# Counting a graph's edges: windows of 64 targets replaced by a stretch of 58 keys that moves with the chunks

## The chip, the cores and the metric

The kernel runs on one core of one Trainium2 chip. TensorE multiplies matrices into PSUM, VectorE and ScalarE work on tiles in SBUF and PSUM, GpSimd fills constants and issues some of the transfers, SyncE issues most of them. The metric is the device time of one execution in microseconds.

## The reference

There are 625 nodes with 1024 features and 20,000 edges, sorted by their target `dst`; each edge has a source `src` and one of two types. A relational graph layer is followed by a layer of routed experts:

```python
n   = t5_norm(layernorm(x)) * ln_weight
out = n @ W_root + bias
for r in range(2):
    sums = segment_sum((n[src] @ W_rel[r]) * (type == r), dst)
    cnt  = segment_sum(type == r, dst)
    out  = out + sums / max(cnt, 1)
x = x + layernorm(x) + elu(out) @ wo
x = x + experts(layernorm(x))    # 2 shared, top 2 of 8 routed, hidden 256
```

## The kernel before

The kernel gathers no edge. It builds the matrix of counts, how many edges of type r run from node s to node d, and multiplies it with the projected nodes. So the graph layer has three parts on TensorE, interleaved in one instruction stream.

**Counting.** The edges go in 160 chunks of 125 (`EC`, `EP`). `edge_columns` (L660 to L688) turns the loaded rows `ety_i`, `dst_i` and `src_i` into columns: it forms the key 640 * type + dst (L663), casts src (L662), transposes both on TensorE (`p_edge`, L669) and lets ScalarE and VectorE write three values of each edge, doubled into pairs, into `cols`: the source within its tile of 125 nodes, the key, and 16 to the power of minus the source's tile. `count_windows` (L823) takes groups of up to four chunks. VectorE makes `ohs` for a group, a one-hot row of 128 columns for each edge's source (L846), times that power (L847), and `ohk`, a one-hot row of keys (L850), by comparison with `iotk`, an iota of 1280 keys. The keys are cut into ten windows of 64 targets, 128 keys with both types (`WD`, `NW`). As edges are sorted by target, `BAND` names for each chunk the one or two windows that its targets can be in, with a slack of 384 edges. For each chunk and window TensorE loads the chunk's `ohs` as weights and adds `ohk` into the window's PSUM bank `cnt` (L859). When a window is complete, `count_out` (L803) scales it to integers on ScalarE (`xi`), splits the five source tiles packed in each number by a mask on VectorE (`ct`, L808), and casts them to bf16 on ScalarE into `CT` (L812, one copy for each type).

**Projecting.** `to_columns` transposes the normalised rows of a tile (`p_t`, L787) into `nT`. `project` (L875) multiplies a tile by one of three weights: 8 k-steps, which the profile records as 16 matmuls (`p_pr`, L880). The first five calls make the root part; the other ten are split into three bf16 parts each in `P` (ScalarE L884 and L887, VectorE L888). These need `stats` (L745) and `scales` (L763), the layernorm of a tile.

**Aggregating.** `aggregate(d, r)` (L893) multiplies `CT` and `P` for target tile d and type r, 15 matmuls (`p_agg`, L898), followed by a short chain on ScalarE and VectorE (L900 to L904); `elu(d)` and `elu_columns(d)` (`p_elT`, L929) prepare it for `output_proj` (`p_y`, L941 and L945).

**The order of the work.** After each chunk, `between(c)` emits what the table `after` (L971 to L1002) lists: projections, aggregations and the rest have chunk numbers written out by hand. A scheduler then orders each engine's instructions by its own estimate of when they become ready, and `tc.issue_after` holds an instruction behind another one of its engine. Each engine works through its own list in order. Ahead of the counting stand 24 and 40 warm-up matmuls (`warm`, L959) and, on GpSimd, in the order of the source: `ident`, the iotas `iota` (L558) and `iotk` (L562), more constants, the small loads `cb`, `vec`, `rb_t`, `bd` and `rw_t` (L609 to L645), and the memsets of `P` and `zero`. Eight buffers of `ohs` and `ohk` let VectorE run ahead of TensorE.

PSUM has eight banks: five for `acc` (windows and projections) and three for `mm`.

Behind the graph layer come `gate`, `route`, the experts and the output; they read only the node rows.

Of the kernel before, what the change touches and what calls it, by code (L numbers as in the profile page):

```python
# [11 lines left out]
I32 = mybir.dt.int32  # L12
# [18 lines left out]
WD = 64  # L31
NW = 10
ND = NW * WD
SH = 313
PACK = 4096
ROUND = 1.5 * 2.0**23
SLACK = 384
BAND = [
    (max(0, (EP * c - SLACK) >> 11), min(NW - 1, (EP * c + EP - 1 + SLACK) >> 11))
    for c in range(EC)  # L40
]
# [411 lines left out]
def sparse_kernel(  # L453
# [32 lines left out]
    psum = ctx.enter_context(tc.tile_pool(name="psum", bufs=1, space=bass.MemoryType.PSUM))  # L486
# [6 lines left out]
    def ps_acc(name):  # L493
        return psum.tile([128, 512], F32, tag="acc", name=name, bufs=5)

    def ps_mm(name):
        return psum.tile([128, 512], F32, tag="mm", name=name, bufs=3)
# [52 lines left out]
    for r in range(R):  # L550
# [5 lines left out]
    KEYS = R * ND  # L556
# [3 lines left out]

    iotk = fbig.tile([128, KEYS], F16, name="iotk")
    nc.gpsimd.iota(iotk, pattern=[[WD, NW], [ND, R], [1, WD]], base=0, channel_multiplier=0,  # L562
                   allow_small_or_imprecise_dtypes=True)
# [92 lines left out]

    SP_, KW_, VV_ = range(3)
    cols = fbig.tile([EP, 3, EC, 2], F16, name="cols")

    def edge_columns():  # L660
        rowf = fbig.tile([EH, 2, 2 * EP], F32, name="rowf")
        nc.vector.tensor_copy(rowf[:, 0], rows_i["src"])  # L662
        nc.vector.scalar_tensor_tensor(rowf[:, 1], rows_i["ety"], float(ND), rows_i["dst"],  # L663
                                       op0=ALU.mult, op1=ALU.add)
# [137 lines left out]
    CT = cbig.tile([TP, NT, KEYS], BF16, name="CT")  # L802
    def count_out(w, acc):  # L803
        xi = crow.tile([TP, R * WD], I32, tag="xi", name=f"xi_{w}")
        nc.scalar.activation(xi, acc[:TP, : R * WD], AF.Copy, scale=256.0)
        five = [TP, NT, R * WD]
        ct = crow.tile(five, I32, tag="ct", name=f"ct_{w}")
        nc.vector.tensor_tensor(ct, xi[:, None, :].to_broadcast(five),  # L808
                                mask[:, :, None].to_broadcast(five), op=ALU.bitwise_and)
        for r in range(R):  # L810
            o = CT[:, :, r * ND + w * WD : r * ND + (w + 1) * WD]
            nc.scalar.copy(o, ct[:, :, r * WD : (r + 1) * WD])  # L812


    GROUP = 4
    groups = []
    for c in range(EC):
        if groups and len(groups[-1]) < GROUP and BAND[groups[-1][0]] == BAND[c]:
            groups[-1].append(c)
        else:  # L820
            groups.append([c])

    def count_windows(between):  # L823
        accs = {}
        for cs in groups:
            c0, g = cs[0], len(cs)
            lo, hi = BAND[c0]
            kn = (hi - lo + 1) * 128
            oh_s = oneh.tile([EP, GROUP, 128], F16, tag="oh_s", name=f"ohs_{c0}")
            oh_k = oneh.tile([EP, GROUP, 256], F16, tag="oh_k", name=f"ohk_{c0}")  # L830

            def both(what, n):
                return [EP, g, n // 2, 2], cols[:, what, c0 : c0 + g][:, :, None, :].to_broadcast([EP, g, n // 2, 2])

            def halves(v):
                return v.rearrange("p g (a b) -> p g a b", b=2)

            order = ExitStack()
            if c0 == 0:
                order.enter_context(tc.issue_after(ahead.ins))  # L840
            elif c0 == 2 * GROUP:
                order.enter_context(tc.issue_after(second[0].ins))
            shape, key = both(SP_, 128)
            row = iota[:EP].rearrange("p (a b) -> p a b", b=2)
# [3 lines left out]
            shape, key = both(KW_, kn)  # L848
            row = iotk[:EP, lo * 128 : lo * 128 + kn].rearrange("p (a b) -> p a b", b=2)
            nc.vector.tensor_tensor(halves(oh_k[:, :g, :kn]), row[:, None].to_broadcast(shape), key,  # L850
                                    op=ALU.is_equal)
            order.close()
            for i, c in enumerate(cs):
                for w in range(lo, hi + 1):
                    first = c == 0 or BAND[c - 1][1] < w
                    last = c == EC - 1 or BAND[c + 1][0] > w
                    if first:
                        accs[w] = ps_acc(f"cnt_{w}")
                    nc.tensor.matmul(accs[w][:, : R * WD], oh_s[:, i, :],  # L859
                                     oh_k[:, i, (w - lo) * 128 : (w - lo + 1) * 128],  # L860
                                     start=first, stop=last)
                    if last:
                        count_out(w, accs.pop(w))
                between(c)

# [27 lines left out]
    def aggregate(d, r):  # L893
        p = ps_mm(f"p_agg_{d}_{r}")
        at = r * ND + d * TP
# [102 lines left out]
    for d, cs in enumerate(((70, 117), (78, 121), (106, 128), (138, 146))):  # L998
        for r in range(R):
            at(cs[r], aggregate, d, r)  # L1000
        at(cs[1], elu, d)
        at(cs[1] + 8, elu_columns, d)  # L1002

    def between(c):
        for f, args in after[c]:
            if f is to_columns:
                args = (args[0], hs[args[0]], *args[2:])
            f(*args)

    count_windows(between)  # L1010
    front.close()

# [10 lines left out]
    for s in range(NT + 2):  # L1023
# [15 lines left out]
        if s == 0:  # L1039
            elu_columns(NT - 1)  # L1040
# [460 lines left out]
```

## Time and profile before

| | us |
|---|---|
| three timed runs, median (lowest to highest) | 310.69 (310.52 to 311.41) |
| the profiled execution, own time | 312.2 |
| its span, first to last instruction | 310.0 |
| TensorE busy, matmuls | 297.6 (96%) |
| VectorE busy | 180.7 (58%) |
| ScalarE busy | 110.1 (36%) |
| first matmul of the counting / of the gate | 9.49 / 141.77 |

In the page's table of slices a digit is an engine's busy share in tenths of 1/40 of the span (7.75 us). In a timeline a row gives the start, the duration, the engine, the line, the operation, the tiles written and read, the number of instructions merged into it, and in brackets the idle time ahead and what ended it. Matmuls are pipelined: the time between the starts of two of them is less than the duration that is shown for one. A row of a group in the page has total busy time, then the mean duration in ns, then the idle time of the engine ahead of the group's instructions with what ended it.

### The profile page before, as it was taken

The page shows a single profiled execution, that of the slowest core. Times are in us where ns is not written, and L with a number is a line of the kernel's source. Part 1 is how long each engine was busy: PE and PEld are TensorE (multiplying, and loading weights), DVE is VectorE, ACT ScalarE, POOL GpSimd, SP SyncE. Part 2 cuts the span into 40 slices and gives each one's busy share as a digit, 9 for nine tenths or more (in the row PEclk, how much of TensorE's full clock was granted, in tenths as well). Part 3 has the DMA queues.
Part 4 walks back from the last instruction along what each step waited for, and adds up shares of the span by engine and source line. Part 5 has one row for each costly group of instructions (what it writes and reads, how often), then busy time and mean ns, then how long its engine had stood idle before and what let it go on. Part 6 is the DMA issues. An engine that isn't in the chain of part 4 may idle for free.

```text
span 310.0 us, 4844 instructions
## 1 busy us (share of the span) xinstructions
PE 297.6 (96%) x1693; PEld 200.9 (65%) x1693; DVE 180.7 (58%) x541; ACT 110.1 (36%) x248; POOL 46.7 (15%) x98
## 2 busy tenths in 40 slices
PE   8799999999999999999999999999999999999991
PEld 7577777887888763456777798877854334444451
DVE  4899999977879676873895032122214211256920
ACT  3456123432436245333424145456459421000000
POOL 9600000000000012431112032120002232200000
PEclk9999999999999999999999999999999999999999
DMA  7999900000000499999999843421047555579351
GB/s 235 306 317 401 406 31 0 3 0 2 0 0 2 126 345 303 388 390 388 319 342 408 349 147 127 137 76 62 0 135 305 218 209 200 201 285 374 154 161 45
DMA packets 27409, 61.18 MB, mean 197 GB/s; under 512 B 2175, under 2 KB 16006, under 8 KB 27374
## 3 DMA queue, kind: packets, MB, share of 16 engines
q1 hardware_dynamic: 21806, 43.77, 39.8%
q0 software_dynamic: 5280, 16.69, 14.9%
q10 hardware_dynamic: 294, 0.35, 0.5%
q8 instruction: 16, 0.26, 0.4%
q14 instruction: 13, 0.11, 0.1%
HBM read 42.76 MB, written 18.81 MB: 199 GB/s over the span
## 4 chain that ended last, share of the span: by engine, by line
PE 78%; DVE 14%; DMA 3%; ACT 1%; issue 1%; SPq 1%; ACTq 0%
PE p_h L1337 12%; PE p_yj L1395 12%; PE p_pr L880 11%; PE p_o L1450 11%; PE p_sh L1115 10%; PE p_y L941 5%; PE p_agg L898 4%; DMA xh<-in_x_dram 3%; PE p_x L1318 3%; DVE ohk L850 2%; PE p_t L787 2%; DVE ohs L847 2%; DVE ohs L846 2%; PE cnt L859 2%; PE p_y L945 1%; DVE ct L808 1%
## 5 line engine op out<-in xcount | busy, mean ns | idle before, releaser
L880 PE MATMUL p_pr<-wg,nT 128*125 128x286 f32 x240 | 61.9, 408 | 0.0
L880 PEld LDWEIGHTS p_pr<-wg,nT 128*125 128x125 f32 x240 | 43.4, 187 | 11.9 <-ACT nT L793 0.4
L1337 PE MATMUL p_h<-w1a,xsT 128*128 (+2 forms) x176 | 40.0, 380 | 0.0
L1395 PE MATMUL p_yj<-w2a,hjT 128*128 (+2 forms) x88 | 38.6, 594 | 0.0
L1450 PE MATMUL p_o<-sw,shT 128*125 128x512 f32 (+1 forms) x88 | 36.1, 553 | 0.0
L1115 PE MATMUL p_sh<-h2T,sw 128*128 128x313 f32 (+1 forms) x128 | 35.2, 428 | 0.0
L1337 PEld LDWEIGHTS p_h<-w1a,xsT 128*128 128x128 f32 (+2 forms) x176 | 28.7, 168 | 7.4 <-issue 0.5
L1115 PEld LDWEIGHTS p_sh<-h2T,sw 128*128 128x128 f32 x128 | 23.7, 189 | 8.6 <-issue 0.2
L1395 PEld LDWEIGHTS p_yj<-w2a,hjT 128*128 128x128 f32 (+2 forms) x88 | 14.4, 168 | 22.4 <-issue 22.1
L1450 PEld LDWEIGHTS p_o<-sw,shT 128*125 128x125 f32 x88 | 16.4, 187 | 16.9 <-issue 16.2
L1399 DVE COPY ys<-p_yj 128x512 f32<-128x512 f32 x15 | 10.4, 692 | 28.7 <-PE p_yj L1395 27.1
L1341 DVE COPY hj<-p_h 128x256 f32<-128x256 f32 x11 | 4.7, 425 | 31.1 <-PE p_h L1337 31.1
L850 DVE TENSOR_TENSOR ohk<-iotk,cols 125x512 f16<-125x512 f16 (+4 forms) x49 | 22.3, 455 | 0.0
L846 DVE TENSOR_TENSOR ohs<-iota,cols 125x512 f16<-125x512 f16 (+3 forms) x49 | 18.2, 372 | 6.5 <-PE cnt L859 6.5
L898 PE MATMUL p_agg<-P,CT 125*125 125x287 bf16 x150 | 20.4, 286 | 0.2 <-DVE P L888 0.2
L955 POOL DMA_DIRECT2D x1d<-xh x10 | 5.3, 533 | 101.6 <-DVE xh L948 101.2
L859 PE MATMUL cnt<-ohk,ohs 125*128 125x128 f16 x223 | 17.9, 219 | 2.8 <-DVE ohs L847 2.8
L859 PEld LDWEIGHTS <-ohs 125*128 125x128 f16 x223 | 14.6, 98 | 7.8 <-DVE ohs L847 4.2
L941 PE MATMUL p_y<-wo_t,eT 128*125 128x512 f32 x40 | 19.2, 603 | 0.0
L898 PEld LDWEIGHTS <-CT 125*125 125x125 bf16 x150 | 18.4, 136 | 0.1
L1403 POOL DMA_INDIRECT yt<-ys,row x11 | 10.8, 984 | 50.5 <-DVE ys L1399 50.5
L847 DVE TENSOR_TENSOR ohs<-ohs,cols 125x512 f16<-125x512 f16 (+3 forms) x49 | 18.1, 369 | 0.0
(295 smaller groups left out, 421.7 us busy)
## 6 DMA issues: line engine op xcount, KB each, us to landing
w1a<-in_L_ffn_W_dram SPq DMA_DIRECT2D x8, 1024.0 KB, 10.9
w2a<-in_L_ffn_W_dram SPq DMA_DIRECT2D x8, 1024.0 KB, 5.1
yt<-zero SPq DMA_DIRECT2D x2, 2560.0 KB
g<-yt SPq DMA_DIRECT2D x10, 512.0 KB, 7.7
sw<-in_L_ffn_sW_dram SPq DMA_DIRECT2D x4, 1024.0 KB, 5.5
x<-x1d SPq DMA_DIRECT2D x5, 500.0 KB
wg<-in_L_gnn_W_rel_dram SPq DMA_DIRECT2D x2, 1144.0 KB, 19.6
x1d<-xh POOLq DMA_DIRECT2D x5, 448.0 KB, 6.2
```

The source lines that it names most:

```text
L846: nc.vector.tensor_tensor(os, row[:, None].to_broadcast(shape), key, op=ALU.is_equal)
L847: nc.vector.tensor_tensor(os, os, both(VV_, 128)[1], op=ALU.mult)
L850: nc.vector.tensor_tensor(halves(oh_k[:, :g, :kn]), row[:, None].to_broadcast(shape), key, op=ALU.is_equal)
L859: nc.tensor.matmul(accs[w][:, : R * WD], oh_s[:, i, :], oh_k[:, i, (w - lo) * 128 : (w - lo + 1) * 128], start=first, stop=last)
L880: nc.tensor.matmul(p[:TP, :F], nT[:, k, m * TP : (m + 1) * TP], wg[:, k, r, :], start=(k == 0), stop=(k == KD - 1))
L898: nc.tensor.matmul(p[:TP, : F + 1], CT[:, m, at : at + TP], P[:, m, r, i], start=(m == 0 and i == 0), stop=(m == NT - 1 and i == 2))
L941: nc.tensor.matmul(ps[s][:TP, :], eT[:, k, :], wo_t[:, k, s * 512 : (s + 1) * 512], start=(k == 0), stop=False)
L1115: nc.tensor.matmul(p[:, : z - a], sw1[:, i, k, t * 128 : (t + 1) * 128], h2T[:, k, a:z], start=(k == 0), stop=(k == KD - 1))
L1337: nc.tensor.matmul(p[a:b, :H], xsT[j][:, k, a:b], w1m[j, a][:, 0, k, :] if a else w1a[:, bass.ds(e, 1), k, :], start=(k == 0), stop=(k == ...
L1395: made = nc.tensor.matmul(p[a:b], hjT[:, j, k, a:b], w2m[j, a, k][:, at] if a else w2a[:, bass.ds(e, 1), k, at], start=(k == 0), stop=(k = ...
L1403: sent.append(nc.gpsimd.indirect_dma_start(out=yt, out_offset=bass.IndirectOffsetOnAxis(ap=row[:, j : j + 1], axis=0), in_=y, in_offset=No ...
L1450: nc.tensor.matmul(p[:TP, :n], shT[:, i, k, own], sw2[:, i, k, at], start=(i == 0 and k == 0), stop=False)
```

## The change

- A chunk's keys become 2 * (dst - LOW[c]) + type, where `LOW[c]` is the lowest target that the slack allows in chunk c. They lie in a stretch of 58 (`KR`), so `iotk` goes and `iota` serves both comparisons. The chunk's offset `low` is made in the kernel: an iota on GpSimd and three small operations on VectorE; `edge_columns` subtracts it.
- One-hot rows are made for eight chunks in a call, except in the first four calls, which keep four.
- The counts lie in three PSUM banks, for two, two and one target tiles; a bank holds 250 keys of each tile. A bank is started by a matmul of a zeroed row (`nil`) over all 512 columns. A chunk adds its 58 columns to one bank, or to two where it crosses a border. `count_out` is called when a bank is complete, twice for each tile (63 and 62 targets).
- `CT` is laid out by 625 targets of each type; the copies into it read every second element of `ct`.
- While the counting runs, PSUM has three `acc`, three `mm` and two `cnt` banks; then the pool is closed and opened again with five and three.
- Some chunk numbers of aggregations and elu columns change; the elu columns of tile 3 move behind the counting.

```diff
+LOW = [max(0, (EP * c - SLACK) // DEG) for c in range(EC)]
+SPAN = (EP - 1 + 2 * SLACK) // DEG + 2
+GROUPS = (4,) * 4 + (8,) * 18
...
-    psum = ctx.enter_context(tc.tile_pool(name="psum", bufs=1, space=bass.MemoryType.PSUM))
+    banks_of = ExitStack()
+    psum, nacc = [banks_of.enter_context(tc.tile_pool(name="psum", bufs=1, space=bass.MemoryType.PSUM))], [3]
...
-    iotk = fbig.tile([128, KEYS], F16, name="iotk")
-    nc.gpsimd.iota(iotk, pattern=[[WD, NW], [ND, R], [1, WD]], base=0, channel_multiplier=0,
-                   allow_small_or_imprecise_dtypes=True)
+    KR = 2 * SPAN
...
+    low = fbig.tile([EH, 2, 2], F32, name="low")
+    nc.gpsimd.iota(low[:, 0], pattern=[[EP, 2]], base=-SLACK, channel_multiplier=2 * EP,
+                   allow_small_or_imprecise_dtypes=True)
+    nc.vector.tensor_scalar(low[:, 1], low[:, 0], 1.0 / DEG, 0.5 / DEG - 0.5, op0=ALU.mult, op1=ALU.add)
+    nc.vector.tensor_scalar(low[:, 1], low[:, 1], ROUND, -ROUND, op0=ALU.add, op1=ALU.add)
+    nc.vector.tensor_scalar(low[:, 1], low[:, 1], 0.0, 2.0, op0=ALU.max, op1=ALU.mult)
...
     def edge_columns():
         rowf = fbig.tile([EH, 2, 2 * EP], F32, name="rowf")
+        two = [EH, 2, EP]
+        nc.vector.tensor_tensor(rowf[:, 0].rearrange("c (j p) -> c j p", j=2),
+                                rows_i["ety"].rearrange("c (j p) -> c j p", j=2),
+                                low[:, 1][:, :, None].to_broadcast(two), op=ALU.subtract)
+        nc.vector.scalar_tensor_tensor(rowf[:, 1], rows_i["dst"], float(R), rowf[:, 0],
+                                       op0=ALU.mult, op1=ALU.add)
         nc.vector.tensor_copy(rowf[:, 0], rows_i["src"])
-        nc.vector.scalar_tensor_tensor(rowf[:, 1], rows_i["ety"], float(ND), rows_i["dst"],
-                                       op0=ALU.mult, op1=ALU.add)
...
-    CT = cbig.tile([TP, NT, KEYS], BF16, name="CT")
-    def count_out(w, acc):
...
+    CT = cbig.tile([TP, NT, R * N], BF16, name="CT")
+    def count_out(d, n, acc):
...
+            nc.scalar.copy(CT[:, :, r * N + d : r * N + d + n], ct.rearrange("p t (d r) -> p t d r", r=R)[:, :, :, r])
+
+    nil = fbig.tile([1, 512], BF16, name="nil")
+    nc.gpsimd.memset(nil, 0.0)
+    MAXG = max(GROUPS)
+    ends = [R * TP * min(DB * (b + 1), NT) for b in range((NT + DB - 1) // DB)]
...
-            shape, key = both(KW_, kn)
-            row = iotk[:EP, lo * 128 : lo * 128 + kn].rearrange("p (a b) -> p a b", b=2)
-            nc.vector.tensor_tensor(halves(oh_k[:, :g, :kn]), row[:, None].to_broadcast(shape), key,
+            shape, key = both(KW_, KR)
+            nc.vector.tensor_tensor(halves(oh_k[:, :g, :]), row[:, None, :SPAN].to_broadcast(shape), key,
                                     op=ALU.is_equal)
...
-                for w in range(lo, hi + 1):
...
-                    nc.tensor.matmul(accs[w][:, : R * WD], oh_s[:, i, :],
-                                     oh_k[:, i, (w - lo) * 128 : (w - lo + 1) * 128],
-                                     start=first, stop=last)
+                a, z = R * LOW[c], R * min(LOW[c] + SPAN, N)
+                for b, end in enumerate(ends):
...
+                    if first:
+                        accs.append(psum[0].tile([128, 512], F32, tag="cnt", name=f"cnt_{b}", bufs=2))
+                        nc.tensor.matmul(accs[b], nil[:, :128], nil, start=True, stop=False)
...
+                    nc.tensor.matmul(accs[b][:, f - base : t - base], oh_s[:, i, :], oh_k[:, i, f - a : t - a],
+                                     start=False, stop=last)
...
-    for d, cs in enumerate(((70, 117), (78, 121), (106, 128), (138, 146))):
+    for d, cs in enumerate(((70, 114), (78, 119), (133, 137), (141, 150))):
...
     count_windows(between)
     front.close()
+    banks_of.close()
+    psum[0] = ctx.enter_context(tc.tile_pool(name="psum2", bufs=1, space=bass.MemoryType.PSUM))
+    nacc[0] = 5
...
-        if s == 0:
-            elu_columns(NT - 1)
+        if s < 2:
+            elu_columns(NT - 2 + s)
```

## The prediction

> **What bounds the kernel now.** I read the page's table of slices first: TensorE is at 9 or more tenths in almost every slice, so time is lost or won in TensorE's own queue. Then the timelines of TensorE, VectorE and GpSimd over the first 145 us, the stage that the change touches; the gate (p_gate, 141.8 us) and all behind it stay as they are.
>
> ```profile
> PE   8799999999999999999999999999999999999991
> ...
> DVE  4899999977879676873895032122214211256920
> ...
> L859 PE MATMUL cnt<-ohk,ohs 125*128 125x128 f16 x223 | 17.9, 219 | 2.8 <-DVE ohs L847 2.8
> ```
>
> A matmul's "mean" is latency, so I take pitches, start to start. Groups of cnt matmuls run at 55.8 ns (37 in 2.23 us, 0.22 of it the last one's tail); a projection of 16 records takes 3.91 us; 15 p_agg take 1.87; 8 transposes p_t 0.87. Summed by stretch:
> - 9.5 to 38.8 us: 5 projections 19.55, 40 p_t 4.4, 48 cnt 2.7, p_vec 0.1: 26.7 of 29.3 us, so 2.6 of waits.
> - 38.8 to 94.65: 10 projections 39.1, 5 aggregations 9.35, 123 cnt 6.9: 55.3 of 55.85.
> - 94.65 to 141.8: 52 cnt 2.9, 5 aggregations 9.35, p_elT 1.7, p_y 22.45, p_t 2.0, the closing layernorm chain 6.2: 44.6 of 47.15, so 2.5 of waits.
>
> VectorE is full from 20 to 62 us and the chain of waits often runs through it, but TensorE's queue is full beside it. So count matmuls are worth their pitch, VectorE's work almost nothing, and a later start its whole length less what it fills of the 2.6 us.
>
> **The start.** First the GpSimd, VectorE and TensorE timelines (start us, duration, engine, line):
>
> ```profile
> 1.44 1.34 POOL L562 IOTA iotk<- 128x1280 f16 x1
> ...
> 4.90 0.75 POOL L609 DMA_DIRECT2D cb<-in_L_gnn_conv_bias_dram  x1
> ...
> 9.20 0.36 POOL L618 TENSOR_TENSOR join<-ident 128x32 f32<-128x32 f32 x1
> 12.28 0.55 POOL L624 DMA_DIRECT2D bd<-in_L_ffn_sb_dram  x1 [2.72 <-DMA cb<-in_L_gnn_conv_bias_dram]
> ...
> 13.80 0.95 POOL L645 DMA_DIRECT2D rw_t<-in_L_ffn_rW_dram  x1
> 14.74 0.25 POOL L869 MEMSET P<- 125x30 bf16 x1
> ```
> ```profile
> 3.24 0.41 DVE L663 SCALAR_TENSOR_TENSOR rowf<-ety_i,dst_i 80x250 f32<-80x250 int32 x1 [1.54 <-DMA dst_i<-in_dst_dram]
> 3.58 0.28 DVE L662 CAST rowf<-src_i 80x250 f32<-80x250 int32 x1
> ```
> ```profile
> 1.28 2.74 PE L961 MATMUL scrap<-iota 128*128 128x128 f16 x24 [1.28 <-POOL iota L558]
> 4.00 1.10 PE L669 MATMUL p_edge<-ident,rowf 80*125 80x80 f32 x4
> 5.03 0.23 PE L730 MATMUL p_lnw<-ident,lnw 8*128 8x8 f32 x1
> 5.19 2.41 PE L961 MATMUL scrap<-iota 128*128 128x128 f16 x40
> 9.49 0.40 PE L859 MATMUL cnt<-ohk,ohs 125*128 125x128 f16 x4 [1.89 <-DVE ohs L847]
> ```
>
> The edge keys now need `low`, an iota on GpSimd that the source places after all the small loads. In the instruction order of the changed kernel as built, it stands behind the rw_t load, where the memset of P stood (14.74), and the memset of `nil` behind it. GpSimd works in order, and its bd load still waits for cb's landing. With iotk gone, what precedes moves up by 1.27 us (1.44 to 2.71): cb is issued at 3.63, and, if it again takes 7.38 us until GpSimd goes on, lands at 11.0. From there to the slot are 2.46 us (12.28 to 14.74): `low` starts at 13.5 and ends at about 13.65.
>
> On VectorE the three steps on `low` stand ahead of the key row. Three dependent small operations: 0.195 us each (L709 to L713 start at 123.20, 123.40, 123.59, 123.79), 0.6. The new subtraction (nearest row L663, 0.41, plus about 0.04 for dependence) 0.45, the key again 0.45, the src cast and the handover to TensorE 0.4. So p_edge starts at about 15.55 instead of 4.00: **11.5 us later**. Behind it stand, in order, q, the first statistics, ahead of the first one-hot rows, h, p_t, every projection. All of it moves; nothing on TensorE can be taken ahead but the 64 warm-up matmuls and the two `nil` matmuls.
>
> Ends for the landing: had GpSimd not to wait at all, it would reach bd at 8.3 (9.56 less 1.27), `low` would end at 10.95, and the delay would be 8.8; if cb lands at 12.28 as before, 12.8. I keep 11.5, since the GpSimd loads from 4.9 to 8.7 us, 4 bytes to 140 KB, all took 6.4 to 7.2 us.
>
> The Trainium skill, "DMA: Bandwidth & Descriptors", section "Anatomy of one DMA — SWDGE (gpsimd) path", gives about 2.0 us plus bytes/436e3, an estimate of 2.3 us for cb; the trace shows 7.1, so the trace decides. By the page GpSimd would not wait and the total below would be 313.1.
>
> **TensorE's pace after the gap.** The first 24 scrap matmuls have a pitch of 108 ns ((2.74 - 0.25)/23), the later 40 of 56: TensorE starts at half pace and is at full pace by 5.19, having lost half of 3.9 us. Now all 64 run ahead, to about 6.6 us, then TensorE idles until 13.7, has a microsecond of work there, and idles again until 21. Does it return to half pace? No row decides: the longest gap here, 2.06 us, did not do it. Ends 0 and +2.0; I take **+2.0**, the gap being three times the one that was harmless.
>
> The Trainium skill, "TensorE: Matmul & The Clock Gate", section "What's actually happening", says that one idle window of about 3.4 us halves the clock and a busy one restores it. An estimate by that page loses half of 3.4 to 6.8 us, 1.7 to 3.4, for a total of 315.5 to 317.2. It speaks against this change, and no run here shows it.
>
> **Early waits: -2.2.** When work starts at 21 us, more of x has landed (st waited 1.09 us for x) and VectorE has less per chunk. Walking the first five projections through the built order, the evictions and statistics stay ahead of TensorE. Ends 0 and -2.6.
>
> **Count matmuls: -7.6.** Before, 223 x 55.8 ns = 12.4 us. Now 160 chunks and 16 that cross a bank: 176, of 58 columns or fewer. Two rows frame them: p_tok, 128 weights and 11 columns, 25.8 ns ((0.40 - 0.168)/9); p_load, 125 weights and 8 columns, about 58.
>
> ```profile
> 150.86 0.43 PE L1143 MATMUL p_load<-sel,ones 125*125 125x8 f16 x5
> ...
> 159.65 0.40 PE L1228 MATMUL p_tok<-oj,oh 125*128 125x11 f16 x10
> ```
>
> The new matmul has 128 weights like p_tok and cnt, so 26 ns: 4.6 us, and 0.2 for the one `nil` matmul inside the stage. At 58 ns the saving is 2.0. Ends -7.7 and -2.0.
>
> **VectorE: about 22 us less work, nearly all hidden.** ohk falls from 22.3 us to 18 x 0.40 + 4 x 0.27 = 8.3 (its rows fit 0.15 us + 0.52 ns an element); the two ohs passes from 36.3 to 2 x (18 x 0.68 + 4 x 0.42) = 27.8. The cover is TensorE's full queue, above. Only the first ohk lies on the path: 0.15 us off the start, inside the rounding. If the 58-wide rows lost the fast rate, ohk would take twice that, still within 4.1 us per projection.
>
> **The end of the counting: +1.4.** ct, xi and CT keep their number (10, 10, 20) but come four at a time. Bank 0 (chunk 67) has two projections ahead of its first aggregation: hidden. Bank 1 ends at chunk 131, right behind aggregation (1,1); call its end T. In the built order all remaining counts follow, about 1.4 us, then the transposes of elu 0 and 1, then the aggregations of tile 2. ScalarE and VectorE do two xi, two ct (0.75 apart) and four CT copies (0.37 apart) ahead of elu 1's exponential: ct ends at T+2.9, the tile 1 sum at 3.35, the exponential at 4.55, the transpose can start at 5.05. TensorE stands from 1.9 to 5.05, and again 0.5 for elu 2: 3.9 with small ones. Before, 43 counts and an aggregation lay in these gaps. Later gaps (0.4 to 0.8 at p_elT) go, as six aggregations now cover the last counts. 3.9 - 2.5 = +1.4; ends -2.5 and +2.5. CT's copies read every second element, unseen here: between today's 0.46 us and twice that, where two copies (0.9) would show. Reopening PSUM's banks costs nothing to 1.0 (the eviction rows L900 to L904); I take nothing, since aggregation (3,1) runs ahead of tile 4's.
>
> **Sum:** +11.5 + 2.0 - 2.2 - 7.6 + 1.4 = **+5.1**. The profiled execution took 312.2 us (span 310.0) and goes to 317.3; on the median of the runs, 310.69, that is **315.8 us**. Loads for the later stages have 20 us and more of slack against p_sh and p_h.
>
> **Rivals.**
> 1. *VectorE was the real bound* (other side). The chain gives VectorE 14%, 43 us; if these held TensorE back, 22.5 of the 58.6 us of one-hot work less would give 0.38 x 43 = 16.5, and 299. For it: VectorE at 100% from 20 to 62 us. Against: only 0.55 us of 55.85 unaccounted on TensorE there. It decides if more than some 6 us of TensorE's time between 9.5 and 141.8 is hidden waiting beyond the 5.6 that I count. 0.09.
> 2. *The start is less late*: GpSimd isn't held by cb and TensorE stays at full pace: 8.8 - 2.2 - 7.6 + 1.4 = +0.4, 311.1, no change. 0.08.
> 3. *Small matmuls don't shrink*: 58 ns as for p_load: +10.7, 321.4. 0.09.
> 4. *The delay doesn't exist*, the key row being ready by 4.5 us: 0.5 - 7.6 + 1.4 = -5.7, 305.0. The built order excludes it unless GpSimd works out of order. 0.02.
>
> Forecast: 0.72. Range 311.0 to 321.0: it takes in rival 2 and the ends of landing and pace, and stops short of rivals 1, 3 and 4, 0.20 in all. About 0.3% (0.9 us) is what a measurement of this kernel can tell from no change. Faster 0.11 (rivals 1 and 4), same 0.08 (rival 2), slower 0.81.
>
> **What would show it.** `low` starting near 13.5 us on GpSimd behind rw_t; p_edge near 15.5; the first cnt near 21 instead of 9.5; cnt groups at 26 ns; a stand of about 3 us at p_elT for tile 1; p_gate near 147 instead of 141.8, and the same 168 us after it. I am wrong if `low` comes before 8 us, if p_gate precedes 141 in spite of it, or if the part behind the gate changes.

## The result, and the profile after

The changed kernel takes **324.79 us** (median of 4 runs, 324.10 to 325.15) against 310.91 before (4 runs, 310.52 to 311.41): 1.0449 times the time, with an interval of 1.0426 to 1.0471. The forecast was 315.8 with a range of 311.0 to 321.0: slower was right, but by 13.9 us and not by 5.1. The profiled execution took 324.1 us (span 322.3; before 312.2 and 310.0).

The page's table of slices of the changed kernel (TensorE, VectorE and the clock that TensorE was granted):

```profile
PE   7149999999997879999999999999999999999991
...
DVE  1359999988536655887488312122214221146920
...
PEclk9658999999999799999999999999999999999998
```

A slice is 8.06 us here. In the second and third slices the row PE has 1 and 4, where the kernel before had 7 and 9: TensorE is nearly idle from 8 to 16 us and half idle to 24, at 6 and 5 tenths of its clock. A second dip stands in the 13th to 15th slices (97 to 121 us), with a clock of 7 tenths in the 14th. VectorE is at nine tenths or more in the fourth to eighth slices (in the third to seventh before) and has less to do behind them. So there are two places to look at. The first, on GpSimd, VectorE and TensorE (start us, duration, engine, line):

```profile
10.69 0.53 POOL L621 DMA_DIRECT2D bd<-in_L_ffn_sb_dram  x1 [2.73 <-DMA cb<-in_L_gnn_conv_bias_dram]
...
12.17 0.93 POOL L642 DMA_DIRECT2D rw_t<-in_L_ffn_rW_dram  x1
13.11 0.16 POOL L655 IOTA low<- 80x2 f32 x1
...
13.71 1.01 POOL L995 MEMSET zero<- 128x1024 f32 x1
```

```profile
13.30 1.45 DVE L657 TENSOR_SCALAR low<-low 80x2 f32<-80x2 f32 x1 [10.83 <-POOL low L655]
14.78 0.17 DVE L658 TENSOR_SCALAR low<-low 80x2 f32<-80x2 f32 x1
```

```profile
13.77 1.03 PE L866 MATMUL cnt<-nil 1*128 1x512 bf16 x2 [6.22 <-POOL nil L824]
16.43 1.13 PE L677 MATMUL p_edge<-ident,rowf 80*125 80x80 f32 x4 [1.63 <-DVE rowf L672]
...
21.78 0.38 PE L868 MATMUL cnt<-ohk,ohs 125*128 125x58 f16 x4 [4.03 <-DVE ohs L850]
...
24.05 5.59 PE L891 MATMUL p_pr<-wg,nT 128*125 128x286 f32 x16
```

GpSimd issues cb at 3.41 us and stands 2.73 us for its landing; `low` comes behind rw_t, at 13.11. VectorE's first step on it takes 1.45 us, the next ones 0.17. The key is transposed at 16.43 instead of 4.00, the first counts run at 21.78 instead of 9.49. TensorE's gaps of 6.2 and 4.0 us show in brackets, and the first projection takes 5.43 us (24.05 to 29.48, start to start) instead of 3.91.

The second place, TensorE at the end of the counting:

```profile
101.18 1.33 PE L868 MATMUL cnt<-ohk,ohs 125*128 125x2 f16 x43
...
106.06 0.86 PE L940 MATMUL p_elT<-ident,el 125*128 125x125 f32 x3 [3.19 <-DVE el L928]
106.72 6.86 PE L909 MATMUL p_agg<-P,CT 125*125 125x287 bf16 x45
114.30 0.51 PE L940 MATMUL p_elT<-ident,el 125*128 125x125 f32 x3 [0.73 <-DVE inv L913]
...
117.87 3.94 PE L909 MATMUL p_agg<-P,CT 125*125 125x287 bf16 x30 [1.19 <-DVE agg L915]
```

43 counts take 1.33 us (27.4 ns each, less the last one's tail): the narrow matmul did what it should. Then TensorE stands 3.19 us for tile 1's elu, 0.73 for tile 2's and 1.19 for a PSUM bank, and 45 p_agg that take 5.75 us at full pace take 6.86. The gate starts at 153.67 instead of 141.77, and behind it the part to the end is as it was (168.6 against 168.2 us).

### The profile page after: what moved, and what is told of

It reads as the page before. It is cut to its first block, busy times and chain, and to the rows that moved or that the text cites. A ratio compares the mean times of both kernels' runs of the same rounds, so it can differ in the third digit from the quotient of the medians.

```text
span 322.3 us, 4679 instructions
## 1 busy us (share of the span) xinstructions
PE 296.1 (92%) x1649; PEld 199.4 (62%) x1649; DVE 170.5 (53%) x464; ACT 107.9 (33%) x246; POOL 45.4 (14%) x99
## 4 chain that ended last, share of the span: by engine, by line
PE 85%; DVE 6%; DMA 2%; ACT 2%; POOL 2%; issue 1%; POOLq 0%; ACTq 0%
PE p_pr L891 17%; PE p_h L1352 12%; PE p_yj L1410 12%; PE p_o L1465 11%; PE p_sh L1130 10%; PE p_y L952 5%; PE p_agg L909 5%; PE p_x L1333 3%; PE p_t L795 2%; DMA cb<-in_L_gnn_conv_bias_dram 2%; PE p_y L956 2%; PE cnt L868 2%; DVE st L757 1%; PE p_hT L1364 1%; PE p_elT L940 1%; PE p_gate L1078 1%
## 5 line engine op out<-in xcount | busy, mean ns | idle before, releaser
L891 PE MATMUL p_pr<-wg,nT 128*125 128x286 f32 x240 | 63.4, 416 | 0.0
L891 PEld LDWEIGHTS p_pr<-wg,nT 128*125 128x125 f32 x240 | 44.5, 191 | 12.1 <-ACT nT L801 0.2
L1352 PEld LDWEIGHTS p_h<-w1a,xsT 128*128 128x128 f32 (+2 forms) x176 | 28.7, 168 | 7.4 <-issue 0.5
L1414 DVE COPY ys<-p_yj 128x512 f32<-128x512 f32 x15 | 10.4, 692 | 28.7 <-PE p_yj L1410 27.1
L909 PE MATMUL p_agg<-P,CT 125*125 125x287 bf16 x150 | 21.1, 297 | 1.4 <-DVE agg L915 1.2
L909 PEld LDWEIGHTS <-CT 125*125 125x125 bf16 x150 | 19.5, 143 | 1.8 <-DVE agg L915 1.5
L952 PE MATMUL p_y<-wo_t,eT 128*125 128x512 f32 x40 | 18.3, 595 | 0.0
L1325 POOL DMA_INDIRECT xs<-h2d,tok x11 | 11.1, 1013 | 45.0 <-PE p_x L1333 30.9
L1367 ACT ACTIVATE hjT<-p_hT,vT 128x128 f32<-128x128 f32 (+2 forms) x34 | 8.7, 332 | 24.2 <-PE p_hT L1364 24.2
L1337 DVE COPY xsT<-p_x 128x512 f32<-128x512 f32 x11 | 7.6, 692 | 17.0 <-PE p_x L1333 14.8
L849 DVE TENSOR_TENSOR ohs<-iota,cols 125x1024 f16<-125x1024 f16 (+1 forms) x22 | 14.0, 636 | 4.6 <-PE cnt L868 4.6
L1441 DVE SCALAR_TENSOR_TENSOR x<-p_o,x 125x512 f32<-125x512 f32 (+1 forms) x11 | 6.9, 640 | 16.3 <-PE p_o L1467 16.3
## 6 DMA issues: line engine op xcount, KB each, us to landing
w1a<-in_L_ffn_W_dram SPq DMA_DIRECT2D x8, 1024.0 KB, 11.9
```

The source lines that it names most:

```text
L849: nc.vector.tensor_tensor(os, row[:, None].to_broadcast(shape), key, op=ALU.is_equal)
L891: nc.tensor.matmul(p[:TP, :F], nT[:, k, m * TP : (m + 1) * TP], wg[:, k, r, :], start=(k == 0), stop=(k == KD - 1))
L909: nc.tensor.matmul(p[:TP, : F + 1], CT[:, m, at : at + TP], P[:, m, r, i], start=(m == 0 and i == 0), stop=(m == NT - 1 and i == 2))
L952: nc.tensor.matmul(ps[s][:TP, :], eT[:, k, :], wo_t[:, k, s * 512 : (s + 1) * 512], start=(k == 0), stop=False)
L1325: nc.gpsimd.indirect_dma_start(out=xs, out_offset=None, in_=h2d, in_offset=bass.IndirectOffsetOnAxis(ap=tok[:, j : j + 1], axis=0))
L1352: nc.tensor.matmul(p[a:b, :H], xsT[j][:, k, a:b], w1m[j, a][:, 0, k, :] if a else w1a[:, bass.ds(e, 1), k, :], start=(k == 0), stop=(k == ...
```

## The experiments

Theory: the loss is (a) the place of `low` in GpSimd's queue with the slow clock behind it, and (b) the end of the counting, where TensorE now has nothing to do while VectorE and ScalarE finish sums, elus and count matrices. Rivals: the new counting itself is slow; VectorE is the bound throughout; and, for (b), that the waits are VectorE's own chains and would turn up elsewhere however TensorE's gaps are filled. Medians are of each kernel's runs; the kernel before measured 310.7 to 311.2 beside them.

### The start

**e1, `low` early.**

```diff
     nc.gpsimd.iota(iota, ...)
+    low = fbig.tile([EH, 2, 2], F32, name="low")
+    nc.gpsimd.iota(low[:, 0], pattern=[[EP, 2]], base=-SLACK, ...)
+    nil = fbig.tile([1, 512], BF16, name="nil")
+    nc.gpsimd.memset(nil, 0.0)
...
-    low = fbig.tile([EH, 2, 2], F32, name="low")
-    nc.gpsimd.iota(low[:, 0], pattern=[[EP, 2]], base=-SLACK, ...)
...
-    nil = fbig.tile([1, 512], BF16, name="nil")
-    nc.gpsimd.memset(nil, 0.0)
```

> The changed kernel with `low`'s iota and `nil` with its memset issued by GpSimd right behind the iota of the compare row, ahead of everything that follows the DMA of cb. My theory is that the late start is all GpSimd's queue: `low` came out at 13.3 us instead of about 2, so the first count matmul should move from 21.8 back to about 9.5 to 10.5, the granted clock should be 1.00 in 8 to 34 us instead of 0.56 and 0.85, p_pr(0) should take 3.9 us instead of 5.4, and the time should fall from 324.8 by 12.3 less the 1 to 2 us of early waits on the one-hot rows that come back, and by the 2.4 of the slow clock: 311 to 313 us. The 5 us behind the last counts would stay. Rival: something else also holds the start (the three key windows, the loads of the edge rows): then p_edge stays behind 8 us and the time above 316.

Measured: 311.31 us (309.95 to 311.57), 1.0008 times the time before (0.9994 to 1.0022). In the change, moving two GpSimd instructions is worth 13.5 us. TensorE's timeline of this kernel:

```profile
4.53 1.09 PE L679 MATMUL p_edge<-ident,rowf 80*125 80x80 f32 x4 [0.51 <-DVE rowf L674]
...
10.31 0.29 PE L868 MATMUL cnt<-ohk,ohs 125*128 125x58 f16 x4
...
11.57 4.12 PE L891 MATMUL p_pr<-wg,nT 128*125 128x286 f32 x16
```

p_edge starts at 4.53 us, the first counts at 10.31, and the first projection runs at full pace (from 0 to 34 us the clock is 1.00). This profiled execution is the fastest of the ten runs, with a mean clock of 0.991; the others have 0.981 to 0.987 and take 310.75 to 311.57 us (see the last section). The end of the counting is unchanged, with the same 3.19, 0.73 and 1.19. The theory of the start holds.

**e2, only the late start, in the kernel before.**

```diff
+    low = fbig.tile([EH, 2, 2], F32, name="low")
+    nc.gpsimd.iota(low[:, 0], pattern=[[EP, 2]], base=0, channel_multiplier=2 * EP, ...)
+    nc.vector.tensor_scalar(low[:, 1], low[:, 0], 0.0, 0.25, op0=ALU.mult, op1=ALU.add)
+    nc.vector.tensor_scalar(low[:, 1], low[:, 1], ROUND, -ROUND, op0=ALU.add, op1=ALU.add)
+    nc.vector.tensor_scalar(low[:, 1], low[:, 1], 0.0, 2.0, op0=ALU.max, op1=ALU.mult)
...
-        nc.vector.scalar_tensor_tensor(rowf[:, 1], rows_i["ety"], float(ND), rows_i["dst"], ...)
+        nc.vector.tensor_tensor(rowf[:, 0]..., rows_i["ety"]..., low[:, 1]..., op=ALU.subtract)
+        nc.vector.scalar_tensor_tensor(rowf[:, 1], rowf[:, 0], float(ND), rows_i["dst"], ...)
```

> The kernel before, counts and one-hot rows as they were, with only the late start put in: an iota `low` on GpSimd in the place that the change gives it, the same three small DVE operations on it (they make it zero), and a subtraction of it ahead of the key; a small addition to the work, and the computed values are the same. If the late start and the clock that it leaves behind are the bulk of the loss, the time is 310.9 + 12.3 + 2.4 less 1 to 2 us of waits that the early one-hot calls no longer cause: 323 to 325 us. If the loss needs the new counts (the 58-key windows, eight chunks a call), it is 313 or less.

Measured: 325.03 us (324.44 to 325.75), 1.0436 (1.0412 to 1.0460). The old counts with the new start lose as much as the whole change does. (The first counts run at 23.05 us here, 1.3 later than in the change, since GpSimd still makes `iotk` first.) So in the change itself the gain of the counts is eaten by something else, (b).

**e3, the gaps filled with warm-up matmuls.**

```diff
-        nc.tensor.transpose(p[:, :KD], lnw, ident[:KD, :KD])
+        made = nc.tensor.transpose(p[:, :KD], lnw, ident[:KD, :KD])
...
+        return made
...
-    warm(24)
+    warm(24 + 190)
     behind = edge_columns()
-    transpose_lnw()
-    warm(40)
+    with tc.issue_after(transpose_lnw().ins):
+        warm(66)
```

> The changed kernel with 190 more warm matmuls ahead of the key's transpose and 66 instead of 40 behind p_lnw, so that TensorE has no gap of 6.2 and 4.0 us ahead of the first counts; nothing else differs, and the first counts stay at 21.8 us. If the idle gaps are what halves the granted clock (0.50 to 0.56 in 8 to 24 us), it reads 1.00 there, p_pr(0) takes 3.9 instead of 5.4 us and the time falls by about 2.4, to 322.4. If the clock is low for another reason (the load from DMA and VectorE together), it stays at 0.5 and the time at 324.8.

Measured: 322.03 us (321.56 to 324.06), 2.8 less than the change. The windows of the trace from 16 to 34 us, first of the change, then of e3 (start, end and length, busy time and instructions of PE, PEld, DVE, ACT, POOL, then the granted clock, the share of the DMA engines and GB/s):

```profile
16.00:22.00 6.00, 1.54 (x9) 1.31 (x9) 4.15 (x15) 2.05 (x4) 0.00 (x0) 0.50 1.06 298
22.00:24.00 2.00, 2.00 (x16) 1.84 (x13) 0.59 (x3) 0.75 (x4) 0.00 (x0) 0.50 1.11 370
24.00:34.00 10.00, 10.00 (x51) 7.79 (x49) 9.39 (x30) 4.24 (x10) 0.00 (x0) 0.85 1.03 403
```

```profile
16.00:24.00 8.00, 7.09 (x91) 6.42 (x92) 5.98 (x18) 3.23 (x8) 0.00 (x0) 1.00 1.07 312
24.00:34.00 10.00, 10.00 (x62) 8.00 (x61) 9.93 (x38) 5.02 (x13) 0.00 (x0) 1.00 1.03 393
```

The clock reads 0.50 up to 24 us and 0.85 behind it in the change, 1.00 in e3: it was slow because TensorE stood, and the step was worth 2.4 to 2.8 us, where I took 2.0.

**e4, GpSimd idle behind `low`.**

```diff
-    nc.gpsimd.memset(nil, 0.0)
+    nc.vector.memset(nil, 0.0)
...
-        nc.gpsimd.memset(zero, 0.0)
+        nc.vector.memset(zero, 0.0)
...
-    nc.gpsimd.memset(P[:, :, :, :, F:], 0.0)
+    nc.vector.memset(P[:, :, :, :, F:], 0.0)
...
-        nc.gpsimd.memset(P[:, m, :, 0, F:], 16.0 ** -m)
+        nc.vector.memset(P[:, m, :, 0, F:], 16.0 ** -m)
```

> The changed kernel with the memsets of nil, of P's last column and of zero on VectorE, where they run in its idle time of the first 13 us, so that GpSimd does nothing behind `low`. The first DVE operation on `low` took 1.45 us, its two like ones 0.17, and it ended in the same moment as GpSimd's memset of zero (14.72). If GpSimd's memset holds VectorE up, the operation now takes about 0.17 us, the first counts come 1.3 us earlier and the time is about 323.5. If the first operation behind a long wait is slow in itself, it stays at 1.45 and the time at 324.8.

Measured: 322.15 us (321.79 to 323.63). VectorE's timeline:

```profile
14.28 0.17 DVE L657 TENSOR_SCALAR low<-low 80x2 f32<-80x2 f32 x1 [10.93 <-POOL low L655]
```

0.17 us instead of 1.45: GpSimd's memsets did hold VectorE's operation up. That the time fell by 2.6 and not by 1.3 is not explained by it; in the profiled execution, the slowest of the five, cb landed 1.0 us later than in that of the change, and the first counts came only 0.24 us earlier. With the change's queue, GpSimd goes on behind cb at 10.41 to 11.67 us in the six profiled executions that have it, so single executions differ by a microsecond there.

### The counts and VectorE's work

**e12, 96 columns a chunk instead of 58, with `low` early.**

```diff
-SPAN = (EP - 1 + 2 * SLACK) // DEG + 2
+SPAN = 48
```

> The kernel with `low` and `nil` early (311.3 us), with 96 columns a chunk in place of 58, the additional ones holding keys that no edge of the chunk has or zero counts. By the two pitches measured (27.4 ns at 58 columns, 55.8 at 128) a matmul of 96 takes 42.8 ns, 15.4 more, for some 180 matmuls. If the counts stand on TensorE's path by their pitch, as I took for the gain of 7.6 us, the time rises by about 2.8, to 314.1. If the gain of the narrow matmuls was hidden, it stays within 1 us.

Measured: 313.16 us (312.53 to 314.77), 1.85 more than e1. Nine counts of 96 columns between two projections take 0.55 us where nine of 58 take 0.42, so a matmul costs about 15 ns more; with 184 of them (eight more cross a bank) that is about 3.0 us. From `p_vec`, near 38 us, to the end of aggregation (1,1), where no wait of note stands in either, e12 takes 51.70 us and e1 50.15: 1.55 more, for 103 counts at 43 ns against 99 at 28, which is 1.7. About two thirds of the 3.0 show in the whole time; p_elT's wait got 0.3 shorter, and the rest I cannot place. The width is paid on TensorE's path, so the forecast's saving of 7.6 was nearly all real: 223 of 55.8 ns against 176 of 27.4 to 28.7, less 0.3 for `nil`, are 7.2.

### The end of the counting

**e5, tile 4's aggregations ahead of the pool's end.**

```diff
     front.close()
+    for r in range(R):
+        aggregate(NT - 1, r)
+    elu(NT - 1)
+    check()
     banks_of.close()
...
-            for r in range(R):
-                aggregate(NT - 1, r)
-            elu(NT - 1)
-            check()
```

> The changed kernel with the aggregations of tile 4, its elu and the check of the counts put ahead of the end of the counting pool, so that p_agg(4,0) takes its PSUM bank from the pool that is open, by turns, and not one of a reopened pool. If the wait of 1.19 us that stood ahead of p_agg(4,0) on the aggregate of DVE is the reopened pool's, it goes and the time falls from 324.8 by 1.0 to 1.2, to 323.7. If it is a true wait for data or for a bank, it stays, and so does the time.

Measured: 325.02 us (323.70 to 325.61): no gain. TensorE's timeline:

```profile
106.36 8.00 PE L909 MATMUL p_agg<-P,CT 125*125 125x287 bf16 x45
...
121.44 0.20 PE L704 MATMUL p_deg<-deg,onec 125*1 125x10 f32 x2 [0.25 <-ACT deg L911]
122.55 2.81 PE L952 MATMUL p_y<-wo_t,eT 128*125 128x512 f32 x6 [0.92 <-PE p_deg L704]
```

The wait at p_agg(4,0) is gone, but 0.25 and 0.92 us stand at the first instructions that follow the reopening, p_deg and p_y. So the wait belongs to the reopened pool, and whatever comes first behind it pays. In both kernels it ends within 0.1 us of VectorE's last read of the old pool, the aggregate (L915): 117.82 and 117.87 us in the change, 122.46 and 122.55 here. (The 45 p_agg took 8.00 us in this execution: see the last section.)

**e6, tile 1's transpose later.**

```diff
         if d < NT - 2:
-            at(cs[1] + 8, elu_columns, d)
+            at(cs[1] + 8 if d != 1 else 141, elu_columns, d)
```

> The changed kernel with the transpose of tile 1's elu behind chunk 141 instead of behind chunk 127, with the counts of the chunks between ahead of it. Theory: the transpose stood 3.19 us for the elu because the counts between take 0.4 us where they took 0.8, and the gap slowed the clock (0.83) of the 45 matmuls of p_agg behind it from 5.6 to 6.9 us. So 2.5 to 3.2 us of the wait go (some may turn up at the next transpose) and about 1.3 with the clock: 320.3 to 321.2 us. Rival: VectorE's chain of aggregate and elu paces this stretch, the wait only moves to the next p_elT or p_agg: 324 us or more.

Measured: 323.12 us (322.22 to 324.77), 1.7 less, under half of the 3.6 to 4.5 expected. The wait only moved: 1.73 us now stand at p_agg for `CT`, which ScalarE has not cast yet, and 1.72 at tile 2's p_elT.

**e7, `low` early with the edits of e5 and e6.** No further edit.

> The changed kernel with `low` and `nil` early, tile 4's aggregation ahead of the pool's end, and tile 1's transpose behind chunk 141 (the first of these runs and the two beside this one). Early `low` alone gave 311.3 us; if the two waits at the end of the counting are separate, 1.2 and about 4.0 more go: 305.5 to 306.5 us, 1.5% under the kernel before. Rival: the end of the counting is paced by VectorE, and the waits return elsewhere: 309 us or more.

Measured: 310.14 us (307.22 to 312.53), 0.9946 (0.9920 to 0.9972). Only 1.2 less than e1; the waits are 1.73, 2.04 and, behind the reopening, 0.25 and 0.92.

**e8, the same with four chunks a call.**

```diff
-GROUPS = (4,) * 4 + (8,) * 18
+GROUPS = (4,) * 40
```

> As the kernel with all three mended, but with one-hot rows made for four chunks a call throughout, as before the change. The calls for eight saved VectorE about 8 us of busy time here (0.41, 0.27 and 0.42 for four chunks against 0.68, 0.39 and 0.68 for eight, 18 times). If VectorE's work is hidden beside TensorE, as I priced it, the time is that of the kernel with all three mended, within 0.5 us. If VectorE is the bound in this stage, it is 3 to 8 us longer.

Measured: 313.95 us (312.43 to 315.31), 3.8 more than e7. From `p_vec` (38 us) to the end of aggregation (1,1), both take 50.2 us (50.26 here, 50.15 in e7): there VectorE's work is hidden, as priced; ahead of it, one wait of 0.62 us for `ohk` shows here. Behind it this kernel has 1.76 and 2.71 us of waits for `CT`, and 0.71 for `ohs`, and its clock fell twice (30 p_agg in 5.58 us and not 3.94). So VectorE's work counts at the end of the counting, and hardly before.

Up to here the rival for (b) looked good: waits moved and did not go. The next three give TensorE real work for the gaps.

**e9, the pool closed behind the output projections, with `low` early.**

```diff
     front.close()
-    banks_of.close()
-    psum[0] = ctx.enter_context(tc.tile_pool(name="psum2", ...))
-    nacc[0] = 5
...
     gnn.close()
+    banks_of.close()
+    psum[0] = ctx.enter_context(tc.tile_pool(name="psum2", ...))
+    nacc[0] = 5
```

> The kernel with `low` and `nil` early (311.3 us), and the counting's PSUM pool closed not behind the counts but behind the output projections, so that the output projections of tile 0 take their banks from the pool that is open. In the kernel before, output projections stood between the last counts (from 100.3 us on); in the changed one they cannot start ahead of the reopening. In the instruction order of this kernel four p_y matmuls stand ahead of the p_elT that waited 3.19 us, one ahead of the next. Theory: the wait at p_elT shrinks by their 1.9 us to about 1.3, the wait of 1.19 at p_agg(4,0) goes, and the slow clock behind the gap (1.2 us) goes too: 307 to 308 us. Rival: the aggregates and elus of VectorE pace this stretch whatever stands between, and what is filled in is lost later for want of banks (three for p_y and not five): 310.5 us or more.

Measured: 310.85 us (310.12 to 312.47). TensorE's timeline, at the end of the counting and ahead of the gate:

```profile
90.14 3.70 PE L952 MATMUL p_y<-wo_t,eT 128*125 128x512 f32 x8 [0.46 <-ACT eT L941]
...
134.11 1.90 PE L797 MATMUL p_t<-ident,h 125*128 125x125 f32 x8 [3.28 <-DVE h L733]
136.68 3.56 PE L1078 MATMUL p_gate<-h2T,rw_t 128*32 128x125 f32 x64 [0.67 <-ACT h2T L805]
```

Eight records of p_y fill the gap at p_elT and the clock holds (45 p_agg in 5.75 us). But now the last p_t stands 3.28 us for the layernorm of tile 4, and the gate's first 64 matmuls take 3.56 us where they took 1.92: what was gained is lost again. In e1, p_sh, work of the shared experts, stood in this gap; it needs the reopened pool too.

**e10, two root projections as filling, with `low` early.**

```diff
-    for i, c in enumerate((7, 15, 21, 24, 28, *range(34, 72, 8), *range(74, 114, 9))):
+    slots = (7, 15, 21, 24, 28, *range(34, 72, 8), *range(74, 114, 9))
+    for i, c in zip((0, 1, 2, *range(5, 15)), slots):
         at(c, project, i)
+    LATE = ((3, 121), (4, 128))
+    for i, c in LATE:
+        at(c, project, i)
```

> The kernel with `low` and `nil` early (311.3 us), and two of the five root projections, those of tiles 3 and 4, moved from chunks 24 and 28 to chunks 121 and 128, the others moving up a place; the pool is reopened as in the changed kernel. Each is 3.9 us of TensorE's work that nobody needs before the sums of tiles 3 and 4, and now stands where TensorE waited. Theory: the wait of 3.19 us at p_elT goes and TensorE keeps its pace behind it (1.2 us), the waits on the last counts shrink: 306.5 to 308 us. Rival: taking them out earlier brings waits on the one-hot rows there, as VectorE is then late: 310 us or more.

Measured: 308.41 us (308.12 to 309.15), 0.9916 (0.9899 to 0.9932). The 3.19 is gone; 1.66 (`CT`), 1.74 (p_elT) and 1.19 (the reopening) are left, and the clock stays at 1.00.

**e11, e9 and e10 together.** No further edit.

> `low` and `nil` early, the pool closed behind the output projections, and the two root projections moved: all of the two kernels beside this one. If what each fills is separate, the wait at p_agg(4,0) goes as well: 305 to 307 us. If one filling is enough, it is that of the better of the two, within 0.5 us.

Measured: 309.05 us (307.89 to 309.88), 0.6 more than e10: no wait is left at the end of the counting, but the last p_t stands 3.3 us, as in e9.

So either any border in the PSUM pools is a wall for what could fill TensorE's gaps, wherever it is put, or VectorE's chains set the end. Three kernels without a border (three `acc` banks to the end, the two count banks unused behind the counting):

```diff
-    psum, nacc = [banks_of.enter_context(tc.tile_pool(name="psum", ...))], [3]
+    psum, nacc = [ctx.enter_context(tc.tile_pool(name="psum", ...))], [3]
...
-    banks_of.close()
-    psum[0] = ctx.enter_context(tc.tile_pool(name="psum2", ...))
-    nacc[0] = 5
```

**e13, on the change alone.**

> The changed kernel, start and all, with one edit: the counting's PSUM pool is not closed and reopened, so that three banks serve p_y and all later `acc` tiles, and not five, and the two count banks stay unused behind the counting. In the instruction order p_y of tile 0 now stands between the p_elT, and p_sh ahead of the last p_t. If the border is a wall for filler work, the 1.19 at p_agg(4,0), 2 of the 3.19 at p_elT and the slow clock behind it (1.3) go and nothing comes back at the last p_t: 320.5 to 321.5 us. If VectorE's chains set the end, the wait moves on and the time stays at 324 or more. If three banks are too few for the experts, the part behind the gate grows from 168.6 us.

Measured: 321.20 us (319.85 to 321.80), 1.0318 (1.0296 to 1.0340): 3.6 less than the change. The waits at p_elT and at p_agg(4,0) and the slow clock are gone; the part behind the gate grew to 170.2 us, as the third case of the expectation has it.

**e14, with `low` early.**

> The same without the border, and `low` and `nil` early as well (311.3 us with the border). Wall: 307 to 308 us. VectorE's chains: 310.5 or more.

Measured: **306.48 us** (305.89 to 307.17), 0.9852 (0.9835 to 0.9869), 4.8 less than e1. TensorE's timeline, to be held against that of the change above:

```profile
89.93 3.70 PE L952 MATMUL p_y<-wo_t,eT 128*125 128x512 f32 x8 [0.46 <-ACT eT L941]
...
93.78 5.75 PE L909 MATMUL p_agg<-P,CT 125*125 125x287 bf16 x45
...
100.89 5.75 PE L909 MATMUL p_agg<-P,CT 125*125 125x287 bf16 x45
```

Eight records of p_y stand where TensorE stood for tile 1's elu, and both groups of 45 p_agg run at full pace. From there to the gate only 0.46 us at p_y and 0.64 at the last p_t are left. The gate starts at 134.9 us, 6.9 earlier than before. Behind the gate 1.4 us are lost in one wait at p_h, put down to "issue". e13, e14 and e15 all have it and no kernel with five banks there has; that it comes of the three banks is likely by this, but no run tests it.

**e15, with the two root projections moved as well.**

> `low` and `nil` early, no border, and the root projections of tiles 3 and 4 at chunks 121 and 128. With the border the two root projections alone gave 308.4 us, with 1.7, 1.7 and 1.2 us of waits left at p_agg, p_elT and p_agg. Wall: these go as they did with the border behind the output projections, and p_sh covers the closing layernorm: 304 to 306 us. VectorE's chains: 308 or more.

Measured: 307.08 us (306.48 to 307.98), 0.9875 (0.9856 to 0.9895). No gain over e14: p_y had filled the gaps already. The rival of e10, waits on the one-hot rows where projections were taken out, shows in neither trace. In the profiled execution the clock fell at the start (the first projection takes 5.68 us), and the two runs with a mean clock of 0.996 and 0.997 took 306.78 and 306.48, as in e14.

e13 and e14 confirm the wall. VectorE's and ScalarE's chains are as long there as in the change: the last step of tile 1's elu on VectorE (L928) starts 4.83 us behind the end of aggregation (1,1) in the change and 4.85 in e13. But from that end to the gate the change takes 53.0 us and e13 47.6 (e1 53.0, e14 47.6), since TensorE has other work meanwhile. e14 beats both kernels.

## Why the prediction was wrong, step by step

By the profiled executions the forecast was 317.3 and the measurement 324.1, so the steps are 6.8 us short; the other 2.2 of the 9.0 are that the profiled execution before lay 1.5 over the median that the forecast went by and that of the change 0.7 under its own; no trace shows where in the kernels these lie.

| step | forecast | measured | where from |
|---|---|---|---|
| start | +11.5 | +12.3 | first counts 9.49 to 21.78 |
| pace after the gap | +2.0 | +2.4 | p_t(0) 1.72 for 0.87, p_pr(0) 5.43 for 3.91; e3: 2.8 |
| early waits | -2.2 | -1.0 | p_pr(5) is 12.0 late: 12.3 + 2.4 - 1.7 (48 counts before, 35 after) leaves -1.0 |
| counts | -7.6 | -7.2 | 223 x 55.8 less 176 x 28 ns, less 0.3 for `nil` |
| VectorE's work | 0 | 0 to chunk 131 | e8 |
| end of the counting | **+1.4** | **+5.5** | waits 5.1 and slow clock 1.1, less 0.7 of p_elT waits before |
| not assigned | | -0.1 | remainder of the gate's 11.9 |

- *The start.* Right in mechanism and place: `low` behind rw_t, held by cb (predicted 13.5, came at 13.11). What was missed is the 1.45 us of the first step on `low`, priced at 0.195 by rows that had GpSimd idle beside them. e1 and e2 prove the step from both sides.
- *The pace.* Right, and a little larger; the value was the upper end of my range for it, and should not have been an end.
- *The early waits.* By the same sum, 1.6 of the 2.6 us are left in the change, so 1.0 went where I took 2.2.
- *The counts.* Right to 0.4 us. Rival 3 (no shrinking) is out, rival 4 too.
- *Rival 1* (VectorE the bound) is out up to the last window (e8). *Rival 2* (a start less late at full pace) is out.
- **The failed step is the end of the counting.** The stand at p_elT was forecast at 3.15 and measured at 3.19. What failed is the rest of this step: "Reopening PSUM's banks costs nothing to 1.0 ...; I take nothing" was 1.19 (e5 shows that it is the reopening); "again 0.5 for elu 2" was 0.73; the slow clock behind a gap of 3.2 us, 1.1 (45 p_agg in 6.86 us, not 5.75), was priced for the start and forgotten here; and of the 2.5 us of waits that were to go in exchange only 0.7 were at p_elT; the rest of that remainder of a sum shows as no wait there in the trace. 1.2, 0.2, 1.1 and 1.8, less 0.25 of small stands that did not come, make the 4.1 that are missing. The deeper error: I took the order with the aggregations behind the transposes as given, and did not ask why p_y, which stood between them before, had gone. TensorE's timeline of the kernel before:

```profile
97.72 0.51 PE L929 MATMUL p_elT<-ident,el 125*128 125x125 f32 x3 [0.17 <-DVE el L917]
...
100.25 1.02 PE L941 MATMUL p_y<-wo_t,eT 128*125 128x512 f32 x2
...
101.34 1.93 PE L941 MATMUL p_y<-wo_t,eT 128*125 128x512 f32 x4
103.16 0.51 PE L929 MATMUL p_elT<-ident,el 125*128 125x125 f32 x3
```

In the change the reopened pool keeps p_y behind it. e13 and e14 show what this wall costs: 5.4 and 5.3 us from the end of aggregation (1,1) to the gate, nearly all of the 5.5 of this step, and 3.6 and 4.8 in the whole time.

The range's upper end, 321.0, had room for +12.8 at the start and +2.5 at the end of the counting, but for no slow clock and no lost filling there.

## What to carry to other kernels

Before giving a new instruction a place, read what its engine's queue holds ahead of it: a two-element iota behind the wait for a small load cost 13.5 us here; put first, it let the keys' transpose start at 4.53 us, 0.5 later than before the change. Where an in-order engine's gaps are filled by work from the next stage, closing and reopening a PSUM pool between them was a wall for that work; ask of each gap what stood in it before. A saving on the bound engine (7.2 us of counts) was kept only where the chains beside it still had cover: TensorE got to the end of the counting sooner and stood there.

## What the runs showed of the hardware

**The clock fell behind gaps of 1.2 to 3.2 us, but not each time.** The same 30 p_agg behind a gap of 1.73 us, in two kernels:

```profile
103.91 5.58 PE L909 MATMUL p_agg<-P,CT 125*125 125x287 bf16 x30 [1.73 <-ACT CT L819]
```

```profile
92.41 3.94 PE L909 MATMUL p_agg<-P,CT 125*125 125x287 bf16 x30 [1.73 <-ACT CT L821]
```

5.58 us in e6 (granted clock 0.62 and 0.53 in 104 to 108 us), 3.94 in e7 (1.00). In e8 gaps of 1.76 and 2.71 both slowed 30 p_agg to 5.58; in e7 one of 2.04 and in e10 ones of 1.66 and 1.74 did nothing. Behind gaps of 3.18 to 3.19 us, 45 took 6.78 (e1), 6.86 (the change), 7.39 (e3) and 8.00 (e5), at full pace 5.75. At the start, gaps of 1.24 to 1.36 us ahead of the first counts (e9, e12, e15) were followed by a first projection of 5.54 to 5.76 us instead of 4.1 (the clock reads 0.50 from 12 to 14 us); behind the 1.89 us of the kernel before, it took 4.12. So a gap of 1.2 to 3.2 us carried a price of 0 to 2.3 us that differed between executions. It shows in the wide runs of e7: the three with a mean clock of 0.996 or more took 307.22 to 308.07 us, the six with 0.980 to 0.984 took 310.14 to 312.53.

The Trainium skill, "TensorE: Matmul & The Clock Gate", section "What's actually happening", has a free-running window of about 3.4 us, of which one idle one halves the clock. That the same gap costs in one execution and not in another agrees with it; but here gaps of half a window and less were enough.

**GpSimd's memsets held a small VectorE operation for 1.3 us**: 1.45 us beside them, ending 0.03 us behind the memset of `zero`, 0.17 without (e4); in e2 1.21. The Trainium skill, "SBUF — State Buffer", section "Who interferes with whom", says that VectorE's two-port modes, which `tensor_scalar` can enter, need a port pair shared with GpSimd, which the first to issue holds for its whole instruction while the other waits. The trace agrees, though no run shows that this operation ran in such a mode; it waited through the memsets of `nil`, `P` and `zero`, which followed each other without a gap.
